# Mamba's first product ahead of the last projection, and depthwise taps moved from VectorE to ScalarE, in a convolution-attention-Mamba-expert kernel

## The chip, the core and the metric

The kernel runs on one core of a Trainium2 chip. A core has a matrix engine (PE, its weight loads shown apart as PEld), a vector engine (DVE), a scalar engine (ACT), a general engine (POOL) and a queue engine (SP) that here only issues transfers. Each works through its own instructions in order and waits on semaphores for the others. SBUF is the on-chip memory, PSUM the eight banks into which PE accumulates, and transfers (DMA) run beside the engines. SP and ACT issue plain transfers; POOL also issues accumulating ones (destination += source).

The metric is device time of one execution in microseconds (us). Each version is run several times, and medians are compared.

## The reference, cut to what matters

An image of 64 x 64 positions and 256 channels passes through three residual layers. `_gn` and `_ln_t` are normalisations without weights.

```python
def _L0_conv_ref(x, W1, W3, W5, Wdw, Wproj, temperature):
    qkv = jnp.concatenate([_conv(xc, W1, 0), _conv(xc, W3, 1), _conv(xc, W5, 2)], axis=1)
    qkv = _conv(qkv, Wdw, 1, groups=3 * c)          # depthwise 3 x 3: nine taps per channel
    q, k, v = jnp.split(qkv, 3, axis=1)
    q, k = (l2n(q), l2n(k))                          # 8 heads of 32 channels, 4096 positions
    attn = jax.nn.softmax(jnp.einsum('bhnc,bhmc->bhnm', q, k) * temperature, axis=-1)
    o = _conv(jnp.einsum('bhnm,bhmc->bhnc', attn, v), Wproj, 0)

def _mamba(x, in_proj_w, conv_w, conv_b, x_proj_w, dt_proj_w, dt_proj_b, A_log, Dp, out_proj_w):
    xc, z = jnp.split(x @ in_proj_w.T, 2, axis=-1)
    xc = silu(causal_conv(xc, conv_w, conv_b))       # 4 taps
    dt, Bm, Cm = split(xc @ x_proj_w.T)              # 16 + 16 + 16
    dt = softplus(dt @ dt_proj_w.T + dt_proj_b)
    h = exp(dt * A) * h + dt * Bm * xc               # a recurrence over 4096 positions
    y = sum(h * Cm) + xc * Dp
    return (y * silu(z)) @ out_proj_w.T

x = x + _L0_conv_ref(_gn(x), ...)
t = t + _L1_attn_ref(_ln_t(t), ...)                  # Mamba forwards + backwards, norm, a two-layer net
t = t + _L1_ffn_ref(_ln_t(t), ...)                   # 2 of 8 experts, gelu, norm
```

All data is float32. Positions are cut into eight chunks of 512, channels into two halves of 128 (`t` or `co`, 0 and 1).

## The kernel before, in words

Four stages follow one another: `conv_phase`, `attention_phase`, `mamba_phase`, `expert_phase`. Nearly all code stands in blocks of `tc.manual_schedule`, in which each engine keeps the order in which Python emits its instructions. Generators are advanced one step at a time (`step`, `drain`), so the order of work is written out by hand. Between two such blocks the compiler merges the engines' two orders, unless an edge between instructions forbids it. A pool (`tc.tile_pool`) hands out a tag's buffers in turn; an instruction that writes a reused buffer waits for the last reader of the old content, a transfer included.

**Convolutions.** k (3 x 3) and v (5 x 5) use Winograd transforms along the width: `inputs` makes the transformed input on DVE, `weights` the transformed weights, which go to DRAM (`uk`, `uv`) and come back as `u`; PE multiplies (L466); `transform_out` brings the products back (`c`, `out_t`, `pad`). q is a plain product (L458). Twelve units (kind, half of the rows, channel half) run in the order k00 k01 k10 k11 q00 v00 q01 v01 q10 v10 q11 v11. Half 0 has 24 output rows, half 1 has 40, since the lower half takes nine rows over from the upper (`edge`, ACT copies at L769 and L807).

`weights(kind, co, dy, r)` takes one row of taps `r` (five times 128 x 256 for v). For v it runs 15 DVE operations of 256 elements in three yields, in tiles of the pool `tp` (six buffers, tag "t"): one for sums `s`, three for results. POOL stores each result pair (L308). The same six buffers serve `c` (L495), the squares `sq` of the norms (L605), `qo` and `vs`.

`depthwise(kind, half, t, pad)` does the nine taps of one unit, in two blocks of rows of 12 (768 elements) or 20 rows (1280). Tap 0 of both blocks is an ACT operation (L559). In the first ten units ACT also computes tap 8 of the second block into `spare` (L564), and POOL adds it to the result by an accumulating transfer (L565). The other taps are DVE operations on the same result (L572), 8 in the first block and 7 in the second, one per step. For v, PE transposes each block as soon as it is done (`turn`, L649 and L651). For q and k the norm follows through `later` and `tick`: `norm_sums` (ACT squares, PE sums), `norm_inverse`, `norm_apply`.

The main loop handles unit n's products and, step by step beside them, unit n-1's depthwise taps: at each group of products it steps `main`, lets PE go on (`feed`, at most three products ahead), calls `tick`, steps the depthwise (6 steps a group for k, 5 for v, all 18 in one go for q) and then `share` pieces of transforms (`step_fill`; twelve in one go for q, before the taps).

**Attention.** For each chunk and channel half, 32 blocks of keys: scores (L1050) into one bank (`ps1`) and three banks (`three()`), exponentials on ACT (L1055, L1056), products with v (L987), sums of exponentials on DVE (L967, L969), accumulated by POOL transfers (L977). `turn` sums them over keys (L1001) and divides; `project` does Wproj, adds the input, stores `x1d` and normalises. The last chunk has its own end: sums, reciprocal (L1006), division (L1025), `project` (L945, L948), store (L950).

**Mamba.** 512 slots, each with two decays on ACT (`da`, L1885), an inflow on POOL (`dbx`, L1895), a scan on DVE (L1908) and a product with C (L1913, some on POOL at L1918), then sums on PE (L1948). Slots of 32 make one chunk and direction. `prepare(q)` makes the next chunk's inputs in 35 steps, one per slot; `LATE` sets other counts for the first 32 slots. The first chunk's inputs are made by `start()`: Silu of `xc` (L1598), first product `pd` (L1607), `xd`, four softplus pieces (`soft` L1617 to L1620, `rest` L1625 to L1627, `log`), `dt_piece` (L1461, L1472, L1476), loads of `b`, `c`, `dtr`, `dtxr` on SP. It also loads the last chunk's `x1` by POOL (L1592) and normalises it to `un` (`layer_norm`), the first input of the backward direction. `start` and the slots advance together: `step(begin)` in each of the first slots.

## Time and profile before

| what | us |
|---|---|
| median of 3 runs (lowest, highest) | 3949.72 (3949.47, 3956.82) |
| profiled execution, its own time | 3948.42 |
| its span | 3946.3 |
| PE busy | 3495.0 (89%) |
| DVE busy | 3308.5 (84%) |
| ACT busy | 2645.8 (67%) |
| POOL busy | 1955.5 (50%) |
| attention's first score (L1050) | at 597.2 |
| last product of attention with v (L987) | ends at 1745.2 |
| first scan (L1908) | at 1787.8 |

Times in the trace are us from the span's start. A line of the timeline gives start, duration of the group, engine, source line, operation, output<-inputs, shape and count; in brackets the idle time of that engine before it and what ended the wait. "issue" is a wait for nothing that the profile shows. The busy shares are means over stages with different limits, so they have to be read stage by stage.

### The profile page before, as it was taken

How to read it: one execution, taken by the hardware profiler on the slowest of the kernel's cores; microseconds unless marked ns; L12 is line 12 of the kernel's file. 1: busy time of each engine (PE TensorE's matmuls, PEld its weight loads, DVE VectorE, ACT ScalarE, POOL GpSimd, SP SyncE). 2: the span in 40 equal slices, each digit the busy share in tenths (PEclk: the TensorE clock that was granted, in tenths of full speed). 3: DMA queues.
4: the chain of work that ended last, by engine and by line, in shares of the span. 5: the costliest groups of instructions: out<-in, count | busy, mean ns of one | idle time of the engine just before them, and what ended most of it. 6: DMA issues, size and time to landing. Idle time of an engine off the chain costs nothing. (4 is left out here: it accounts for less than half of the span.)

```text
span 3946.3 us, 41780 instructions
## 1 busy us (share of the span) xinstructions
PE 3495.0 (89%) x14792; PEld 1121.7 (28%) x14792; DVE 3308.5 (84%) x2391; ACT 2645.8 (67%) x4138; POOL 1955.5 (50%) x1422
## 2 busy tenths in 40 slices
PE   6779999999999999998788888889888888876898
PEld 2334432222222222222222222223222222322444
DVE  8997678888888887778999999999999999999222
ACT  1222338988898898877777778777777777775222
POOL 3121001111111111117889899898988889887000
PEclk9989999999999999998899989989988898988999
DMA  6343246665666665563334433443434345342211
GB/s 217 112 132 104 83 143 141 128 129 112 139 120 121 137 121 118 110 146 122 127 120 124 124 126 117 118 128 118 133 119 121 104 122 152 102 130 79 65 62 57
DMA packets 184186, 471.95 MB, mean 120 GB/s; under 512 B 39205, under 2 KB 48677, under 8 KB 183710
## 3 DMA queue, kind: packets, MB, share of 16 engines
q1 hardware_dynamic: 137166, 304.26, 24.9%
q0 software_dynamic: 44496, 156.53, 19.0%
q10 hardware_dynamic: 2304, 8.39, 0.6%
q8 instruction: 118, 1.93, 0.2%
q14 instruction: 102, 0.84, 0.1%
HBM read 268.17 MB, written 79.56 MB: 88 GB/s over the span
## 5 line engine op out<-in xcount | busy, mean ns | idle before, releaser
L1895 POOL TENSOR_TENSOR dbx<-dtxr,b 128x1024 f32<-128x1024 f32 x512 | 1203.1, 2359 | 194.3 <-DVE da L1908 104.4
L1908 DVE TENSOR_TENSOR_SCAN da<-da,state,dbx 128x1024 f32<-128x1024 f32 x432 | 1014.0, 2347 | 15.7 <-ACT da L1885 7.1
L1056 ACT ACTIVATE e<-sc 128x1536 f32<-128x1536 f32 x512 | 740.2, 1446 | 1.3 <-PE sc L1050 1.3
L1885 ACT ACTIVATE da<-dtr,aneg 128x512 f32<-128x512 f32 x1024 | 708.1, 692 | 32.9 <-DMA dtr<-dtd 2.4
L977 POOL DMA_DIRECT2D s<-s x222 | 194.0, 999 | 900.6 <-DVE s L969 523.3
L969 DVE TENSOR_TENSOR s<-s,e 128x2048 f32<-128x2048 f32 x256 | 586.7, 2292 | 44.1 <-ACT e L1056 20.7
L1050 PE MATMUL sc<-q,kS 32*128 32x512 f32 x4096 | 588.3, 639 | 4.6 <-ACT e L1055 3.9
L1913 DVE TENSOR_TENSOR h<-da,c 128x1024 f32<-128x1024 f32 x432 | 529.2, 1225 | 32.5 <-DVE da L1908 0.5
L987 PE MATMUL av<-e,vT 128*32 128x512 f32 x4096 | 545.4, 605 | 2.4 <-DVE o L993 2.4
L1948 PE MATMUL y<-h,sel 128*32 128x512 f32 x2048 | 377.5, 663 | 93.1 <-DVE h L1913 68.1
L466 PE MATMUL cv<-v,u 128*128 128x512 f32 x928 | 410.3, 603 | 37.8 <-DVE pad L287 13.6
L967 DVE TENSOR_TENSOR s<-e 128x2048 f32<-128x2048 f32 x128 | 293.2, 2291 | 127.5 <-ACT e L1056 110.0
L1055 ACT ACTIVATE e<-sc 128x512 f32<-128x512 f32 x512 | 305.9, 597 | 112.8 <-PE sc L1050 58.1
L1341 PE MATMUL mm<-u,win 128*128 128x512 f32 x464 | 243.9, 667 | 69.9 <-ACT z L1449 28.9
L1050 PEld LDWEIGHTS sc<-q,kS 32*128 32x128 f32 x4096 | 163.8, 183 | 430.7 <-ACT e L1055 387.6
L1939 ACT COPY state<-da 128x2 f32<-128x2 f32 x431 | 68.7, 160 | 300.9 <-DVE h L1913 297.4
L466 PEld LDWEIGHTS cv<-v,u 128*128 128x128 f32 x928 | 178.3, 193 | 267.0 <-issue 222.3
L572 DVE SCALAR_TENSOR_TENSOR acc<-pad,wdw_s,acc 128x768 f32<-128x768 f32 (+1 forms) x182 | 224.8, 1240 | 33.3 <-ACT acc L559 27.9
L1387 PE MATMUL mm<-xp,taps 128*128 128x512 f32 x480 | 213.3, 596 | 0.6 <-DVE m L1537 0.6
L1908 DVE TENSOR_TENSOR_SCAN h<-da,state,dbx 128x1024 f32<-128x1024 f32 x80 | 187.5, 2343 | 10.3 <-ACT state L1939 9.3
L987 PEld LDWEIGHTS av<-e,vT 128*32 128x32 f32 x4096 | 80.9, 108 | 390.9 <-issue 376.7
L1918 POOL TENSOR_TENSOR h<-h,c 128x1024 f32<-128x1024 f32 x80 | 188.3, 2353 | 1.0 <-ACT state L1939 1.0
(380 smaller groups left out, 3894.1 us busy)
## 6 DMA issues: line engine op xcount, KB each, us to landing
s<-s POOLq DMA_DIRECT2D x222, 512.0 KB, 6.4
dtr<-dtd SPq DMA_DIRECT2D x128, 512.0 KB
dtxr<-dtd SPq DMA_DIRECT2D x128, 512.0 KB
b<-bcd SPq DMA_DIRECT2D x64, 256.0 KB
c<-bcd SPq DMA_DIRECT2D x64, 256.0 KB
dtd<-dt SPq DMA_DIRECT2D x64, 256.0 KB
dtd<-few SPq DMA_DIRECT2D x64, 256.0 KB
u<-uv SPq DMA_DIRECT2D x24, 640.0 KB
```

The costliest lines, as they stand in the source:

```text
L466: nc.tensor.matmul(rows4(ps), u[:, dy, P * ci : P * ci + P], v[:, dy : dy + HR, ci, :], start=dy + ci == 0, stop=dy == k - 1 and ci == CT - 1,
L967: nc.vector.tensor_tensor(g.part, before, e, ALU.add)
L969: nc.vector.tensor_tensor(g.part, g.part, e, ALU.add)
L987: nc.tensor.matmul(g.av[32 * h : 32 * h + 32, :], vT[:, kb, P * t + 32 * h : P * t + 32 * h + 32], e[:, h, :], start=kb == 0, stop=kb == N ...
L1050: nc.tensor.matmul(sc[1][:, h - 1, :] if h else sc[0], kS[r, t, P * kb : P * kb + P], q_t[r, t, :], start=True, stop=True,)
L1055: nc.scalar.activation(e[:, 0, :], sc[0], AF.Exp)
L1056: nc.scalar.activation(e[:, 1:4, :], sc[1], AF.Exp)
L1885: nc.scalar.activation(da[:, v, :], dts[i, e, j][0][:, v, :], AF.Exp, scale=aneg[i % 2][:, a : a + 1])
L1895: nc.gpsimd.tensor_tensor(u, dts[i, e, j][1], bcs[i, k][0][:, None, :].to_broadcast([P, 2, N]), ALU.mult)
L1908: nc.vector.tensor_tensor_scan(das[n].rearrange("p v n -> p (v n)"), da.rearrange("p v n -> p (v n)"), u.rearrange("p v n -> p (v n)"), st ...
L1913: nc.vector.tensor_tensor(h, da, bcs[i, k][1][:, None, :].to_broadcast([P, 2, N]), ALU.mult)
L1948: nc.tensor.matmul(ys[i, e][32 * j : 32 * j + 32, :], cx.sel, hs[n + j // 2][:, j % 2, :], start=False, stop=k == SQ - 1,)
```

## The change

Three things are changed.

1. In the first ten units `depthwise` hands taps 7 and 8 of both blocks to ACT (`aside`): ACT writes each into a scratch tile (`spare`, and `spare2` or a free part of the result for half 0), POOL accumulates it. The second block's pair goes first, the first block's after its DVE taps. DVE keeps six taps a block. The transposes of v come after both blocks. The edges of q move to DRAM tiles (`q_edges`), stored and reloaded by POOL.
2. `weights` works on two arrays at once (512 elements) where it can. For v that makes ten operations instead of 15, and six buffers instead of four; stores and yields stay three pairs and three.
3. At the end of attention the sums and the last projection use the single bank (`alone()`), and the projection is emitted last. `start()` adds two compile-time edges: the projection's first product comes behind the first softplus product on PE, its first addition behind `dt_piece` on DVE. `pd` uses another bank. Six of the seven steps of `un`'s norm move from before the first slot into the slots, and `LATE` starts `prepare(1)` later. Pool `b_w` is placed before `b_sm`.

```diff
@@ conv_phase
-        edges = {
-            k: one.tile([P, 9, 4, TX], FP, name=f"edge{i}") for i, k in enumerate((0, 1, ("q", 0), ("q", 1)))
-        }
+        edges = [one.tile([P, 9, 4, TX], FP, name=f"edge{t}") for t in range(CT)]
+        q_edges = [cx.rows.tile([P, 9, 4, TX], FP, name=f"q_edge{t}", tag=f"q_edge{t}") for t in range(CT)]
...
         def weights(kind, co, dy, r):
...
+            s, o = two(), two()
             if kind == "v":
-                plus(y, w[1], w[3])
-                plus(x, x, w[4])
-            plus(o[:, 0, :], x, y if kind == "v" else w[1])
-            plus(o[:, 1, :], x, y if kind == "v" else w[1], ALU.subtract)
-            store()
-            yield
...
+                plus(s, r[:, 0:2, :], r[:, 2:4, :])
+                plus(s[:, 0, :], s[:, 0, :], r[:, 4, :])
+                odd = s[:, 1, :]
...
+            plus(o[:, 0, :], s[:, 0, :], odd)
+            plus(o[:, 1, :], s[:, 0, :], odd, ALU.subtract)
+            store(o, (0, 1))
+            yield
...
+            s, odd, o = two(), two(), two()
+            madd(s, r[:, 4::-4, :], 4.0, r[:, 2:3, :].to_broadcast([P, 2, C]))
+            madd(s, s, 4.0, r[:, 0:5:4, :])
+            madd(odd, r[:, 3:0:-2, :], 4.0, r[:, 1:4:2, :])
+            yield
+            for f, points in ((2.0, (2, 4)), (-2.0, (3, 5))):
+                if f < 0:
+                    o = two()
+                madd(o, odd, f, s)
+                store(o, points)
+            yield
...
+            def aside(b):
+                m = mine * W // 2
+                for tap, x in ((7, spare), (8, spare2 if half else dst[:, 2 * m : 3 * m])):
+                    _, src, w_ap = piece(b, tap)
+                    x = x[:, 0:m]
+                    nc.scalar.activation(x.rearrange("p (h w) -> p h w", w=W), src, AF.Copy, scale=w_ap)
+                    nc.gpsimd.dma_start(out=dst[:, m * b : m * b + m], in_=x, accum_op=ALU.add)
             if away:
-                o, src, w_ap = piece(1, 8)
-                x = spare[:, 0 : mine * W // 2]
-                nc.scalar.activation(x.rearrange("p (h w) -> p h w", w=W), src, AF.Copy, scale=w_ap)
-                nc.gpsimd.dma_start(out=dst[:, mine * W // 2 : mine * W], in_=x, accum_op=ALU.add)
+                aside(1)
...
-                for tap in range(1, 8 if b and away else 9):
+                for tap in range(1, 7 if away else 9):
...
-                if kind == "v":
-                    m = mine * W // P // 2
-                    turn(dst, t, row0 * W // P, m * b, m, ("tr", "ps2") if shared else ("tr",))
+                if away and b == 0:
+                    aside(0)
+                m = mine * W // P // 2
+                for part in (range(2) if b else ()) if away else (b,):
+                    if kind == "v":
+                        turn(dst, t, row0 * W // P, m * part, m, ("tr", "ps2") if shared else ("tr",))
...
-                    nc.scalar.copy(pad[:, 0:9, 1:5, :], edge)
+                if half and kind == "q":
+                    nc.gpsimd.dma_start(out=pad[:, 0:9, 1:5, :], in_=q_edges[t])
+                elif half:
+                    nc.scalar.copy(pad[:, 0:9, 1:5, :], edges[t])
...
-                    nc.scalar.copy(edge, pad[:, LAG : LAG + 9, 1:5, :])
+                if not half and kind == "q":
+                    nc.gpsimd.dma_start(out=q_edges[t], in_=pad[:, LAG : LAG + 9, 1:5, :])
+                elif not half:
+                    nc.scalar.copy(edges[t], pad[:, LAG : LAG + 9, 1:5, :])
@@ attention_phase
+        def alone():
+            return ps1.tile([P, N], FP, name="sc1", tag="sc1")
...
-                ps = aside()
+                ps = alone() if c == NCH - 1 else aside()
...
+                    if c == NCH - 1 and co + t == 0:
+                        behind.append(ins)
+                ins = nc.vector.tensor_tensor(x1[:, co, :], xr[:, co, :], ps, ALU.add)
+                if c == NCH - 1 and co == 0:
+                    behind.append(ins)
...
-            den = three()[:, 0, :]
+            den = alone() if g.last else three()[:, 0, :]
...
+            for task in queue:
+                drain(task)
             drain(turning)
-            for task in queue + [project(NCH - 1, oT)]:
-                drain(task)
+            drain(project(NCH - 1, oT))
+    return behind
@@ mamba_phase, start()
-            pd = mm_psum()
+            pd = tl_psum()
...
+            def ahead_of(ins):
+                tc.add_manual_dep(
+                    ins.ins, next(i for i in reversed(nc.cur_bb.bb.instructions) if i.engine == ins.ins.engine).name,
+                    mybir.DependencyInfo(mybir.DependencyClass.NoSync, mybir.DependencyReason.DATA), reason="behind",
+                )
             soft(0)
+            if behind:
+                ahead_of(behind[0])
             rest(0)
             log(0)
             for v in range(2):
                 dt_piece(0, v, 0, ex, nc.vector)
+                if behind and v == 1:
+                    ahead_of(behind[1])
...
-            step(norm)
-            step(norm)
             soft(1)
-            step(norm)
             soft(2)
             rest(1)
             soft(3)
-            step(norm)
...
             inflow(1)
-            step(norm)
             load_bc(0, 3)
             yield
+            step(norm, 3)
...
             step(norm)
-            nc.sync.dma_start(out=ud[NCH - 1], in_=un)
-            drain(norm)
             yield
             dt_piece(0, 0, 2, ex)
             yield
             dt_piece(0, 1, 2)
+            step(norm)
             yield
...
             dt_piece(0, 0, 3, ex)
             yield
+            step(norm)
+            nc.sync.dma_start(out=ud[NCH - 1], in_=un)
+            drain(norm)
             dt_piece(0, 1, 3)
...
-        LATE = {0: 0, 1: 0, 2: 0, 3: 0, 5: 2, 6: 2, 7: 5, 15: 2, 16: 2, 17: 2}
+        LATE = {0: 0, 1: 0, 2: 0, 3: 0, 4: 0, 5: 0, 6: 2, 7: 3, 8: 3, 9: 3, 10: 2, 15: 2, 16: 2, 17: 2}
```

## The prediction

> **What bounds the kernel now.** I read the page's busy shares first, then the busy time by stretch (a stretch from:to, its length, then busy time of PE, PEld, DVE, ACT and POOL, PE's clock, DMA share, GB/s):
>
> ```profile
> 127.00:204.00 77.00, 62.58 (x153) 25.78 (x153) 73.55 (x73) 19.96 (x30) 4.64 (x8) 0.90 0.33 98
> 204.00:274.00 70.00, 53.01 (x127) 21.31 (x126) 62.17 (x91) 19.67 (x30) 19.29 (x34) 0.89 0.46 146
> 274.00:306.00 32.00, 32.00 (x79) 13.29 (x82) 31.27 (x49) 4.83 (x8) 6.53 (x12) 0.94 0.34 122
> 306.00:598.00 292.00, 274.61 (x694) 117.45 (x691) 206.69 (x201) 93.28 (x143) 25.32 (x48) 0.97 0.35 112
> 598.00:1746.00 1148.00, 1140.16 (x8449) 271.03 (x8448) 934.63 (x489) 1016.91 (x1065) 205.17 (x234) 1.00 0.62 125
> 1746.00:1788.00 42.00, 32.16 (x56) 10.11 (x56) 29.64 (x59) 16.95 (x25) 5.88 (x4) 0.76 0.59 203
> 1900.00:3655.00 1755.00, 1465.78 (x4132) 470.98 (x4130) 1690.29 (x1030) 1310.76 (x2580) 1534.48 (x934) 0.90 0.40 119
> ```
>
> So: in the convolutions DVE is the bound up to about 274, with PE idle 14.4 and 17.0 us in the first two rows; from 274 PE is (32.00 of 32, then 274.61 of 292); attention is PE's (1140 of 1148); the scans are DVE's (96%). Between attention and scans lies a fill of 42 us in which nobody is full. Next, PE's timeline over the convolutions: where PE waits, it waits for DVE's evacuations of PSUM.
>
> ```profile
> 126.60 17.98 PE L466 MATMUL cv<-v,u 128*128 128x512 f32 x36 [13.59 <-DVE pad L287]
> ...
> 203.37 5.13 PE L458 MATMUL cv<-xpad,wq 128*128 128x512 f32 x8 [14.42 <-DVE pad L287]
> ...
> 273.82 19.47 PE L466 MATMUL cv<-v,u 128*128 128x512 f32 x40 [9.68 <-DVE out_t L290]
> ```
>
> What DVE does ahead of those evacuations are depthwise taps and weight transforms; its timeline shows a transform held by its own stores, and the 15 taps of unit (k,1,1) in one run:
>
> ```profile
> 230.40 0.76 DVE L287 SCALAR_TENSOR_TENSOR wo<-wx 128x256 f32<-128x256 f32 x2 [1.71 <-DMA uv<-wo]
> ...
> 248.85 23.71 DVE L572 SCALAR_TENSOR_TENSOR acc<-pad,wdw_s,acc 128x1280 f32<-128x1280 f32 x15
> ```
>
> Last the timeline of the fill. Mamba's first product (L1607) has its input by 1748.9 and starts at 1760.43, behind the projection; from there a fixed chain runs to the first scan:
>
> ```profile
> 1750.88 3.36 DVE L1006 RECIPROCAL rs<-sc 128x512 f32<-128x512 f32 x1 [2.74 <-PE sc L1001]
> ...
> 1760.43 3.60 PE L1607 MATMUL mm<-xc,wx 128*48 128x512 f32 x8 [0.87 <-DVE x L948]
> ...
> 1770.91 0.33 SPq L1476 DMA_DIRECT2D dtd<-dt  x1
> ...
> 1781.73 4.87 POOL L1895 TENSOR_TENSOR dbx<-dtxr,b 128x1024 f32<-128x1024 f32 x2 [17.06 <-DMA dtxr<-dtd]
> 1781.81 2.58 DVE L1625 TENSOR_SCALAR few<-ex 128x512 f32<-128x512 f32 x1
> ...
> 1787.80 2.35 DVE L1908 TENSOR_TENSOR_SCAN da<-da,state,dbx 128x1024 f32<-128x1024 f32 x1
> ```
>
> **Part 1: taps to ScalarE.** Ten of twelve units lose 3 of 15 DVE taps: 18 x 1.018 us (768 elements) and 12 x 1.551 us (1280), 36.9 us of DVE. ACT gains 18 x 0.92 + 12 x 1.35 = 32.8 us, POOL 30 issues x 0.89 = 27 us, and 30 more accumulating transfers land. ACT (44 of 179 us busy from 127 to 306) and POOL (30 of 179) have room. Only taps ahead of a PE wait count. Units (k,0,0) and (k,0,1): 3 x 1.02 each, out of the 14.4 us wait, 6.1. Unit (k,1,0): 3 x 1.55 = 4.65, out of the 9.68 wait. Unit (q,0,0) runs where PE is full: nothing; cover is PE's v products, and with it gone it would be worth 3.
>
> Unit (k,1,1) pays part back. Its second block must wait for two accumulations onto the same bytes. The first issues at 249.96 after the weight stores on POOL, and lands 5.8 us later (measured there). If the second waits for it: 0.9 issue and about 5 (the others: 3.8 to 6.6), so 261.6. The first block's six taps end at 248.85 + 6 x 1.58 = 258.3: a stall of 3.3, net gain 4.65 - 3.3 = 1.35. Ends: no waiting between them, gain 4.65; landings of 6.6, gain 0. The Trainium skill, "DMA: Bandwidth & Descriptors", Rules for kernel authors, says that an accumulating DMA must be waited for before another touches the same bytes. The same page, Anatomy of one DMA, puts the fixed cost of any DMA at about 2 us; with 2 in place of 5 for the second landing, the stall would be 0.3 and the total 3 us better. The trace's rows, 3.8 and more, say otherwise.
>
> After 306 PE decides. Its 4.75 us wait at 393 (for DVE's pad) loses two taps of unit (q,0,1): -2. Units (v,0,0), (v,0,1) and (v,1,0) run their taps in one go, under 26 us of PE's v products, and PE's transposes follow. Their two blocks now both end with four accumulations in a row. For (v,1,0): spare at 498.45, then 4 x (0.9 + 5.1) less overlap, lands about 516.5, against transposes that start at 514.74 and today wait 1.95 in the middle: +1 (0 to +5). For the 768 ones 3.8 each, end 336.5 against 341.15: covered with 4.6 to spare.
>
> The q edges go through DRAM: four ACT copies (0.67) off, four POOL issues on. The reload is needed about 5 us after its pad is free; nearest rows land in 2.5 (256 KB stores) and 8.4 us (384 KB loads): 0, up to +3 each. Who waits is ACT's side copies and behind them the taps, under the same 26 us.
>
> **Part 2: weight transforms.** A v transform takes 5.65 us today in 15 operations (0.34 to 0.45 apart at 256 elements). The new one has ten, of them six at 512 (0.60 to 0.68 apart): 5.25. Five for v0 ahead of 126: -2. For v1, four run from 219.5 to 248.85, with 6.1 us of stalls for stores. They share six buffers with the norm's squares, three of which PE holds until 235 (it reads them at 234.18). Today a transform needs four buffers, then six; the last pair can only reuse the one whose store has just left. With stores landing in 2 to 7 us I get +3 and +2 in the first two transforms, -1 in each of the others: +3 (ends: -8, 21 us without stalls; +10, 4 us more in three).
>
> Convolutions: -6.1 - 4.65 - 1.35 - 2 + 3 = -11.1 up to 274, then -2 + 1: **-12** (ends -27 and +4). PE's waits there (13.6 + 14.4 + 9.7 alone) are large enough to give it.
>
> **Part 3: Mamba's start.** L1607 goes behind the softmax sums, which end at 1750.82: 9.6 earlier. Its bank is now that of the attention output, copied out by 1747.7. The 21.3 us from its start to the first inflow on POOL stay: 1772.1, and 2.43 later, at 1774.6, the scan has its inputs. Today it starts 3.6 after that point, since DVE has the last two softplus rests first, slowed from 0.42 to 2.58 and from 0.69 to 2.73 beside POOL. With the projection's two adds (0.69 each) behind dt_piece and the norm's subtraction gone from there, these rests end between 1770 (softplus products ahead of the projection's second half on PE) and 1778 (behind it: that half waits for the first add, as both have one bank). I take 1775.5, near the inputs: 12.3 earlier; ends 9 and 13.2.
>
> What is moved: the projection's eight matmuls (about 4 us) run in PE time free after 1756; its adds cost DVE 1.4 where DVE waits for ACT anyway. The x1 store on SP leaves near 1764.6 instead of 1760.3. POOL's load of x1 waits for it (3.8 today) in front of the first inflow: 1768.4 against 1772.1, so a slip above 3.7 delays the scan one for one. Six of the norm's seven steps go into the slots: subtraction 1.22 on DVE, which is full there: +1.2. Square 1.04 and reciprocal-root row 0.66 on ACT fit its idle 1.9 per slot; pow 1.24 and the product 2.33 on POOL (two inflows ahead), 3.8 on PE and four issues on SP are covered by the scans. Uncovered, POOL's would cost 1.2 (the product is there today). The second direction's preparation starts two slots later, with the same total of 37 steps; today's waits of the first 32 slots (about 10 us, most for ACT's da) move, and I count 0, from -3 to +4. The setup's taps and skips (5.2 us of DVE) have about 5 us of waiting to fall into; uncovered +3.
>
> Mamba: -12.3 + 1.2: **-11** (ends -15 and -4). Afterwards DVE stays the bound, so the shift reaches the end.
>
> **Sum.** -23. The profiled execution took 3948.42 (span 3946.3 and 2.1 around it), 1.3 under the median 3949.72. It would be 3925.4, by the median 3926.7: 3927.
>
> **Rivals.** (a) The convolutions give nothing: v1's buffers and the accumulations eat it (-12 becomes 0 to +2): 3939 to 3941. For: the 6.1 us of store waits already there. Against: (k,0,0) to (k,1,0) have their landings 10 us ahead of need. (b) Mamba's head start is lost, since the compile-time order leaves L1607 behind the projection, or x1's load blocks POOL: -12 and -1 remain: 3937. For: POOL's queue has that load ahead of the inflow. Against: 3.7 us of slack. (c) Slower: the accumulations land later beside one another. Place: the end of (v,0,0), (v,0,1), (v,1,0) before PE's transposes, and (k,1,1). Each us of landing costs 4 in (v,1,0), 4 in the 768 units above their 4.6 of slack, 2 in (k,1,1). Two us more (7 instead of 5) cost 8 + 3 + 3 + 4 = 18, nearly all of the gain; four cost 16 + 11 + 11 + 8 = 46: 3973. It decides from about 2.3 us. For: the landings spread from 3.8 to 6.6 with single transfers. Against: the DMA share is 0.35 there.
>
> **How the numbers follow.** Forecast 0.56 (its own range 3915 to 3938), (a) 0.20, (b) 0.13, (c) 0.11. 0.2% (7.9 us) is about what a measurement tells from no change. Faster: all of the forecast and (b), nearly half of (a) and none of (c): 0.77; same: the rest of (a) and the start of (c), 0.14; slower 0.09. The range takes the forecast's low side with the better ends (no stalls in v1, -40: 3910) and reaches over (a) and (b) to 3948.
>
> **What would show it.** PE's waits at 203 and 273 shorter by 6 and 5 with L572 at 12 per unit; a wait of DVE for DMA inside (k,1,1); the stores' waits in v1; attention's first score near 585 instead of 597. L1607 right behind L1001, the first scan 43 us after the last exp becoming about 31. The prediction is wrong if accumulations wait on each other for longer than 5 us, if PE's transposes of v wait, or if the first 32 slots lose what the start gained.

## The result, and the profile after

The changed kernel takes 3966.01 us (median of 7 runs, 3960.57 to 3970.61), the kernel before, run beside it, 3951.95 us (7 runs). The ratio is 1.0038 with a 95% interval of 1.0029 to 1.0047: 14 us slower, where 23 us faster were forecast. The profiled execution took 3966.26 us with a span of 3964.3, which is 18.0 more than the span of before. Repeated executions of the kernel before lay between 3938.9 and 3957.5 us over all the comparisons below, so single profiles are compared by landmarks inside them, and times by their medians and intervals.

Two landmarks cut the loss in two. The first is attention's first score on PE, where the convolutions end: 597.22 before, 605.43 after (+8.2). The second is the fourteenth scan, from which on all scans keep their distance for 40 and more: 1838.47 before, 1853.54 after (+15.1), of which 7.4 are there already at attention's last run of products (1742.06 and 1749.42). So the convolutions lost 8.2 us instead of gaining 12, and Mamba's start lost 7.7 instead of gaining 11. Later single waits of scans make 15.1 into 18.6 in this one profile; the medians differ by 14.1.

The stretches of the profile after, with the same columns as the prediction's table (busy time of PE, PEld, DVE, ACT and POOL, PE's clock, DMA share, GB/s), their bounds moved with the landmarks:

```profile
125.00:202.00 77.00, 62.31 (x153) 25.85 (x154) 67.74 (x67) 26.04 (x35) 11.25 (x17) 0.90 0.55 142
202.00:275.00 73.00, 54.94 (x127) 22.76 (x128) 55.45 (x66) 21.35 (x29) 22.92 (x38) 0.84 0.56 160
306.00:606.00 300.00, 278.36 (x688) 119.38 (x686) 187.43 (x184) 105.70 (x153) 41.09 (x66) 0.94 0.48 136
1753.00:1785.00 32.00, 18.81 (x40) 5.17 (x40) 25.06 (x58) 13.75 (x20) 2.88 (x2) 0.73 0.68 239
```

DVE did lose work (73.55 to 67.74 us in the first row, 62.17 to 55.45 in the second), but these stretches are no shorter (77 and 70 us before). The work left DVE and the time stayed. The last row shows that the fill between attention and the scans did shrink, from 42 to 32 us.

PE's timeline after, where it waits in the convolutions, and attention's first score. Most of these waits are for an evacuation, the operation on DVE or ACT that reads a finished PSUM bank and so frees it for PE:

```profile
125.27 17.68 PE L470 MATMUL cv<-v,u 128*128 128x512 f32 x36 [11.68 <-DVE pad L286]
...
201.75 6.67 PE L462 MATMUL cv<-xpad,wq 128*128 128x512 f32 x8 [14.42 <-DVE pad L286]
...
262.01 10.71 PE L470 MATMUL cv<-v,u 128*128 128x512 f32 x20 [18.06 <-ACT c L499]
...
522.49 1.09 PE L663 MATMUL ps<-ident,acc 128*128 128x128 f32 x4 [5.98 <-DVE acc L583]
...
605.43 1.12 PE L1075 MATMUL sc<-q,kS 32*128 32x512 f32 x2
```

The wait of 13.6 us shrank by 1.9; that of 14.42 is the same to the hundredth, although six taps of 1.02 were to come out of it. The wait of 9.68 for DVE at 274 is gone, but PE now stands 18.06 us for an ACT copy at 262, and it goes on at 274.70 where it did at 273.82. At 522 there is a new wait of 5.98.

Behind the wait for ACT, in DVE's and ACT's timeline of the profile after:

```profile
230.93 0.69 DVE L286 SCALAR_TENSOR_TENSOR wx<-wx 128x512 f32<-128x512 f32 x1 [4.31 <-DMA uv<-wx]
...
247.47 9.48 DVE L583 SCALAR_TENSOR_TENSOR acc<-pad,wdw_s,acc 128x1280 f32<-128x1280 f32 x6
...
254.55 1.36 ACT L572 ACTIVATE spare<-pad,wdw_s 128x1280 f32<-128x1280 f32 x1 [37.79 <-DMA acc<-spare]
...
260.12 1.36 ACT L572 ACTIVATE spare<-pad,wdw_s 128x1280 f32<-128x1280 f32 x1 [4.21 <-DMA acc<-spare]
260.13 9.55 DVE L583 SCALAR_TENSOR_TENSOR acc<-pad,wdw_s,acc 128x1280 f32<-128x1280 f32 x6 [3.18 <-DMA acc<-spare]
261.39 0.56 ACT L499 COPY c<-cv 128x512 f32<-128x512 f32 x1
```

ACT's tap for the first block must wait until the transfer that still reads the scratch tile has landed. The copy of PE's finished bank (c) stands behind it in ACT's order: PE had that bank ready at 244, ACT copies it at 261.39. The Trainium skill, "PSUM — Partial Sum Buffer", Engine vs sequencer instructions, says that ScalarE's queue is strictly first in, first out; these lines agree.

At 522 it is unit (v,1,0). POOL's and DVE's timeline after:

```profile
500.44 0.89 POOL L573 DMA_DIRECT2D acc<-spare  x1 [5.11 <-ACT spare L572]
506.04 0.88 POOL L573 DMA_DIRECT2D acc<-spare  x1 [4.71 <-issue]
507.69 0.86 POOL L573 DMA_DIRECT2D acc<-spare  x1 [0.78 <-DVE acc L583]
...
512.91 9.55 DVE L583 SCALAR_TENSOR_TENSOR acc<-pad,wdw_s,acc 128x1280 f32<-128x1280 f32 x6 [5.76 <-DMA acc<-spare]
...
517.20 0.86 POOL L573 DMA_DIRECT2D acc<-spare  x1 [8.65 <-DMA acc<-spare]
```

The second accumulation onto the second block is issued 5.60 us after the first, when that has landed, and lands 6.9 us later. Only then do the block's six taps begin, 5.76 us late; they end at 522.46, and PE's transposes start at 522.49. The first block, which PE transposes first, is ready no earlier: its second accumulation is issued at 517.20, when the one ahead of it has landed, and lands 5.2 us later, at 522.4. The profile puts PE's wait down to the taps, but the two ends lie 0.1 us apart. The Trainium skill, "DMA: Bandwidth & Descriptors", Rules for kernel authors, demands that an accumulation waits for the one before it onto the same bytes, and the trace shows it kept.

Last, Mamba's start after, from the timelines of PE, SP, DVE and POOL:

```profile
1757.73 3.63 PE L1634 MATMUL tl<-xc,wx 128*48 128x512 f32 x8
...
1771.27 0.33 SPq L1503 DMA_DIRECT2D dtd<-dt  x1
...
1785.05 2.36 DVE L1943 TENSOR_TENSOR_SCAN da<-da,state,dbx 128x1024 f32<-128x1024 f32 x1 [2.25 <-ACT da L1920]
...
1815.40 2.35 POOL L149 TENSOR_TENSOR un<-ln_xc,ln_rstd 128x1024 f32<-128x1024 f32 x1 [0.29 <-DMA ln_rstd<-ln_inv]
...
1829.26 10.57 PE L1414 MATMUL mm<-xp,taps 128*128 128x512 f32 x24
...
1847.53 2.35 DVE L1943 TENSOR_TENSOR_SCAN h<-da,state,dbx 128x1024 f32<-128x1024 f32 x1 [5.33 <-ACT da L1920]
```

Counted from attention's last run of products, the first product starts 10.0 us earlier than before and the first scan 10.1 earlier. Then the product that makes the norm's result un starts at 1815.40 (1796.22 before), the second direction's products follow in one run of 10.57 us, and the tenth to the fourteenth scan wait for ACT and for PE's y sums. Of the 10.1 us nothing is left by then: 17.8 are lost in fourteen slots, 7.0 of them in the first four scans and 11.0 from the tenth on.

### The profile page after: what moved, and what is told of

It is laid out like the page before. It is cut to its first block, busy times and chain, and to the rows that moved or that the text cites. A ratio compares the mean times of both kernels' runs of the same rounds, so it can differ in the third digit from the quotient of the medians.

```text
span 3964.3 us, 41756 instructions
## 1 busy us (share of the span) xinstructions
PE 3496.7 (88%) x14792; PEld 1124.8 (28%) x14792; DVE 3263.7 (82%) x2301; ACT 2674.3 (67%) x4164; POOL 1985.6 (50%) x1456
## 5 line engine op out<-in xcount | busy, mean ns | idle before, releaser
L583 DVE SCALAR_TENSOR_TENSOR acc<-pad,wdw_s,acc 128x768 f32<-128x768 f32 (+1 forms) x152 | 188.4, 1243 | 65.1 <-ACT acc L564 33.7
```

## The experiments

The first theory, from the traces alone: (A) the convolutions lose through the taps, by two accumulations onto one block; Mamba loses because x1 comes late and the norm, un and the second direction's preparation with it. The rivals are in the expectations. The table gathers the landmarks of all runs: shift of attention's first score and of the fourteenth scan against the profile of before, the latter also counted from attention's last run of products, and the ratio of times to the kernel before.

| run | first score | 14th scan | 14th scan, from attention's end | ratio (95% interval) |
|---|---|---|---|---|
| the change | +8.2 | +15.1 | +7.7 | 1.0038 (1.0029 to 1.0047) |
| e1_taps | +8.0 | +7.1 | +0.2 | 1.0004 (0.9994 to 1.0014) |
| e2_weights | +6.6 | +5.5 | -1.0 | 1.0006 (0.9994 to 1.0017) |
| e3_mamba | 0.0 | +9.7 | +9.4 | 1.0019 (1.0008 to 1.0031) |
| e4_x1_early | +0.9 | +2.6 | +1.2 | 1.0003 (0.9993 to 1.0014) |
| e5_v_single | 0.0 | -2.8 | -1.9 | 0.9993 (0.9983 to 1.0004) |
| e6_pace | +7.7 | +7.3 | -0.9 | 1.0011 (1.0000 to 1.0021) |
| e7_bufs8 | -6.1 | -7.7 | -0.6 | 0.9980 (0.9971 to 0.9990) |
| e8_act_setup | +3.2 | +3.7 | -0.2 | 0.9992 (0.9983 to 1.0002) |
| e9_norm_late | -0.6 | +12.3 | +13.6 | 1.0032 (1.0020 to 1.0045) |
| e10_bufs_only | -0.3 | -0.9 | -0.4 | 0.9993 (0.9984 to 1.0003) |
| e11_bufs8_act | -6.6 | -8.1 | -2.9 | 0.9980 (0.9968 to 0.9991) |
| e12_taps_k | -7.2 | -6.3 | +1.8 | 0.9965 (0.9952 to 0.9978) |
| e13_late_only | +2.1 | +9.0 | +6.9 | 1.0014 (1.0004 to 1.0023) |
| e14_norm_only | -0.5 | +6.9 | +7.4 | 1.0016 (1.0007 to 1.0025) |
| e15_best | -7.9 | -12.8 | -3.7 | 0.9956 (0.9943 to 0.9970) |

Single profiles scatter. The six runs that leave the convolutions as they were (e3, e4, e8, e9, e13, e14) have the first score between -0.6 and +3.2; up to 2.4 us come in before 110 us, where DVE waits for the first weights and their stores (0.80 us of waiting at 83 before, 2.68 in e1_taps). The seven that leave Mamba's start as it was (e1, e2, e5, e6, e7, e10, e12) have the fourteenth scan, counted from attention's end, between -1.9 and +1.8. A single profile does not tell a difference inside these bounds from nothing.

**Parts alone.** e1 is the diff's taps and edges, e2 its `weights`, e3 its hunks in `attention_phase` and `mamba_phase`, each on the kernel before.

> The kernel before with the change's taps alone (two taps of nine per block on ScalarE, the q edges through DRAM); weight transforms and Mamba's start as before. Theory A, read from the two traces: the convolutions lose time through the accumulations (the two onto one block run one after the other, ACT stands still behind its scratch, PE's transposes of unit (v,1,0) wait), so the taps alone move attention's first score from 597.2 to between 604 and 608, and the time rises by 7 to 11 us, to about 3960. Rival B: the weight transforms cost it, with their wide tiles in the buffers shared with the norm; then the taps alone leave the first score at 597 or below, and the time within 2 us of before.

> The kernel before with the change's weight transforms alone. Theory A: PE's first wait in the convolutions goes from 13.6 to about 11.7 us, the transforms of v1 wait as long for their stores as before, and what is left at attention's first score is 0 to 1.5 us earlier than 597.2; the time is 0 to 2 us below before. Rival B (the weight transforms cost the convolutions): first score at 603 or later, time 6 us or more above before.

> The kernel before with the change's Mamba start alone (first product ahead of the last projection, norm steps among the slots, second direction's preparation later). Theory A: the first scan starts 9 to 11 us earlier than 1787.8 and by the fourteenth scan the kernel is 6 to 9 us behind the kernel before (15 to 18 us lost among the first 14 slots), which stays to the end: time 6 to 9 us above before. Rival C: the parts act on each other only together (the convolutions' delay shifts what meets at the start); then the Mamba start alone keeps its gain, and the time is 5 to 10 us below before.

e1 shows what theory A says of the first score, with PE's wait of 6.37 us at 522 again; 2.4 of its 8.0 us are the chance named above, and by the ratio its time is only 1.6 us (-2.4 to +5.5) above before, not the 7 to 11 expected. e2 goes by rival B: the first score is 6.6 late, and DVE waits 11.8 us for stores and 4.4 ahead of the fourth transform (6.1 in all before); its time, too, rises by less than rival B says (2.4 us by the ratio). So both parts move the first score on their own, by separate causes, and both together by no more than one alone. e3 is nearly as theory A expects (the fourteenth scan 9.7 behind instead of 6 to 9, the time 7.5 above by the ratio), and rival C falls.

**x1 early.** On e3: the first x1 add ahead of the softplus, the second behind the dt pieces, the norm's steps a slot earlier, the table LATE of before.

```
+            if behind:
+                ahead_of(behind[1])      # right behind aneg
...
-        LATE = {0: 0, 1: 0, 2: 0, 3: 0, 4: 0, 5: 0, 6: 2, 7: 3, 8: 3, 9: 3, 10: 2, 15: 2, 16: 2, 17: 2}
+        LATE = {0: 0, 1: 0, 2: 0, 3: 0, 5: 2, 6: 2, 7: 5, 15: 2, 16: 2, 17: 2}
```

> The run of the Mamba start alone, with three things put elsewhere: the projection's two adds on DVE go ahead of the softplus (the first) and right behind the first dt pieces (the second), so that the x1 store leaves some 4 us earlier and ahead of the dtr load; the norm's steps are one slot earlier each; the second direction's preparation starts as early as in the kernel before. Theory A (x1 comes late, and through it the norm, un and the preparation): first scan 12 to 14 us earlier than 1787.8, un's product at 1800 or before, fourteenth scan 3 to 8 us ahead of the kernel before, time 3 to 8 us below before. Rival D: the preparation's work on PE and ACT meets the scans wherever x1 is, because the scans now start before it; then the fourteenth scan is 4 us or more behind as in the run of the Mamba start alone, and the time 3 to 8 us above before.

The loss is gone but for 1.2 us, which is inside the scatter; the gain did not come, so neither theory A's range nor rival D's was met. As three things were changed at once, this run cannot say which of them did it; e9, e13 and e14 show what the steps' places cost.

**One tap aside in v units.** The change's taps and weights, Mamba's start as before. In the v units the transposes also go back behind each block:

```
-                for tap in range(1, 7 if away else 9):
+                for tap in range(1, (8 if b else 9) if one_tap else 7 if away else 9):   # one_tap: v units
...
-                if away and b == 0:
+                if away and b == 0 and not one_tap:
                     aside(0)
```

> The change's taps and weight transforms (Mamba's start as before), but the v units keep one tap on ScalarE and one accumulation, as before. Theory A (the taps cost the convolutions through the two accumulations onto one block of v units, which PE's transposes wait for): PE's wait of 6.0 us at 522 falls below 1 and attention's first score, 605.4 with the whole change, comes to between 597 and 600; time about 6 below that of taps and weights together, within 2 us of before. Rival E (the loss lies ahead of that, in the scratch that holds ACT from 254 to 261, and is only collected at 522): the first score stays at 603 or later.

PE's timeline at the transposes of (v,1,0), first of the kernel before, then of e5_v_single, then of e1_taps:

```profile
514.74 0.66 PE L649 MATMUL ps<-ident,acc 128*128 128x128 f32 x4
```

```profile
514.14 0.66 PE L665 MATMUL ps<-ident,acc 128*128 128x128 f32 x4
...
519.18 1.09 PE L665 MATMUL ps<-ident,acc 128*128 128x128 f32 x4 [1.74 <-issue]
```

```profile
521.86 1.09 PE L658 MATMUL ps<-ident,acc 128*128 128x128 f32 x4 [6.37 <-DMA acc<-spare]
```

The transposes start at 514 as in the kernel before, and all 8.2 us are back at the first score. Theory A holds for the convolutions, rival E falls: the scratch holds ACT here too (PE waits 18.87 us at 262), and the first score is that of before. e5 takes away both things that end at 522 in the change, the late taps and the late landing, so it does not say which of them counts; in e1 the profile puts PE's wait down to the landing.

**The pace of the taps.** The change's taps and weights with `-(-12 // groups)` in place of `-(-18 // groups)` in the loop over the units, which is the number of `step(before)` per group.

> The change's taps and weight transforms (Mamba's start as before), with the taps paced at four steps per group of output rows in the k units instead of six (three instead of five in v units). Theory F: the removed taps were the last of each unit, behind PE's waits, and six steps still lie ahead of each evacuation; at four steps PE's wait of 11.7 us at 125 shrinks by about 2 us (2 x 1.02) and that of 14.4 us at 202 by about 3 us (2 x 1.56), so PE reaches 205 some 5 us earlier than with the whole change; the time falls by 0 to 5 us against taps and weights together, since the v transforms behind can take some back. Rival G (PE's waits are not set by the taps ahead of the evacuation but by what the transforms of the output wait for): both waits change by less than 1 us.

PE's timeline of e6_pace:

```profile
194.86 6.42 PE L462 MATMUL cv<-xpad,wq 128*128 128x512 f32 x8 [8.77 <-DVE pad L286]
...
257.62 10.91 PE L470 MATMUL cv<-v,u 128*128 128x512 f32 x20 [20.82 <-ACT c L499]
...
398.99 3.78 PE L470 MATMUL cv<-v,u 128*128 128x512 f32 x4 [8.14 <-ACT pad L793]
...
521.95 1.08 PE L663 MATMUL ps<-ident,acc 128*128 128x128 f32 x4 [6.06 <-DVE acc L583]
```

The wait of 14.42 fell to 8.77 and the one ahead of it from 11.68 to 9.91: theory F, with a larger effect than the 3 us expected of the second. DVE runs a fixed six steps of the unit before ahead of each evacuation, however many taps are left; a shorter unit only ends sooner behind it. Of the 6.9 us at 195 only 4.4 are left at 257, where ACT's scratch takes its share. The rest is gone at 429, ahead of the double accumulation: at 399 PE waits 8.14 us for ACT's copies into `pad`, and these wait 10.04 us for a depthwise tap on DVE. This run slowed the taps in v units as well, to three steps per group, and they now end there.

**Buffers.** e7 is e2 with `bufs=8` instead of 6 in the pool a_t and the q edges through DRAM, for room; e10 is the same on the weight transforms of before.

> The change's weight transforms alone with eight buffers of 2 KB per partition instead of six in the pool they share with the norm; for the room the two q edges go through DRAM as in the change. Theory A2 (the wide tiles wait for their own stores because the pool is small): DVE's waits for stores in v1's transforms, 16.2 us with the weight transforms alone (6.1 in the kernel before), fall to 6 us or less, the six-tap run of unit (k,1,1) starts at 246 or before instead of 255.5, and attention's first score comes to between 590 and 597 instead of 603.8; time 3 to 8 us below before. Rival H (the waits are the stores' own landing time on a loaded queue, and more buffers are used up by the norm's squares): waits of 10 us or more remain, first score 600 or later.

> The kernel before with eight buffers in the shared pool and the q edges through DRAM, and its own weight transforms of 256 elements. Theory A2' (buffers are what v1's transforms lack, and the wide transforms are worth about 2 us of DVE): the waits for stores in v1 fall from 6.1 to below 3 us, attention's first score comes to between 592 and 596 (597.2 before), time 1 to 6 us below before, and some 3 us above the run with wide transforms and eight buffers. Rival J (all of that run's gain is the buffers'): first score 589 to 592, time 6 to 10 us below before.

DVE's timeline in the transforms of v1, first of e2_weights, then of e7_bufs8:

```profile
230.27 0.69 DVE L287 SCALAR_TENSOR_TENSOR wx<-wx 128x512 f32<-128x512 f32 x1 [6.55 <-DMA uv<-wx]
...
239.58 1.29 DVE L287 SCALAR_TENSOR_TENSOR wx<-wx 128x512 f32<-128x512 f32 x2 [4.59 <-DMA uv<-wx]
...
255.54 23.71 DVE L577 SCALAR_TENSOR_TENSOR acc<-pad,wdw_s,acc 128x1280 f32<-128x1280 f32 x15
```

```profile
227.95 0.69 DVE L286 SCALAR_TENSOR_TENSOR wx<-wx 128x512 f32<-128x512 f32 x1 [1.14 <-DMA uv<-wx]
...
233.19 0.69 DVE L289 TENSOR_TENSOR wx<-wr 128x512 f32<-128x512 f32 x1 [4.55 <-DMA wr<-in_w]
...
243.62 23.71 DVE L576 SCALAR_TENSOR_TENSOR acc<-pad,wdw_s,acc 128x1280 f32<-128x1280 f32 x15
```

With two more buffers the waits fall from 16.2 to 5.7 us, most of what is left being the load of the next raw weights, and the taps start 11.9 us earlier. The time falls by 0.20% (0.10 to 0.29): rival H falls. The buffers alone (e10) leave 3.5 us of store waits and move neither the first score nor, beyond its interval, the time: a miss for the expectation of 592 to 596, and rival J falls too. It also has e7's way of the q edges through DRAM, which therefore is not the gain. By the first score, the wide transforms and the buffers are worth something only together (+6.6, -0.3, and -6.1 with both); by time, the intervals of e7 and e10 still overlap.

**Setup on ACT.** On e4: the 24 scaled identities (tap matrices of the second direction, skip matrices) are built by ACT in its gaps instead of by DVE ahead of the softplus.

```
-                nc.vector.tensor_scalar(tp[:, j, :], cx.ident, cx.col(f"convw{d}", j), None, ALU.mult)
+                nc.scalar.activation(taps[1][:, j, :], cx.ident, AF.Copy, scale=cx.col("convw1", j))
```

> The run with x1 early, with the second direction's tap matrices and the skip matrices (24 operations, 5 us of DVE ahead of the softplus) built on ACT in its idle time. Theory A3 (the setup on DVE delays dt, x1 and through them first scan and preparation): against the last attention product, the first scan comes 3 us earlier than in the run with x1 early (from 36.8 us to about 33.5 behind the start of the last run of attention products) and the fourteenth scan 2 to 4 us earlier; time 2 to 5 us below before. Rival D2 (from the fifth scan on the second direction's preparation on ACT and PE paces the scans, whenever they begin): the first scan is 3 us earlier and the fourteenth within 1 us of the run with x1 early.

The first scan came 2.5 us earlier, the fourteenth 1.4: between A3 and D2, though 1.4 is inside the scatter, and the intervals of the times of e4 and e8 overlap. Counted from attention's end, un comes 1.4 earlier too (55.1 us against 56.5), and DVE waits 5.66 us ahead of the sixth scan for an inflow that stands on POOL behind un's product.

**The moves among the slots.** e9 is the kernel before with the change's places of the norm's steps and its table LATE, but the first product behind the projection as before; e13 only the table; e14 only the norm's steps. In e14 the first eight products of the second direction's projection (at 1805.18) read un before the norm's last product has written it (at 1812.12), so their wait for un is missing from its time; the next eight do wait for it.

> The kernel before with the second half of the change's Mamba start alone: the norm's steps among the slots and the second direction's preparation later, while the first product stays behind the projection. Theory A4 (the preparation, which starts from the norm's un, sets the pace from the fifth slot on; the later steps cost about 18 us over 14 slots, from which the head start of 10 is then taken off): the first scan stays within 2 us of 1787.8 or gains up to 6 (the norm is out of its way), un's product ends more than 15 us later than 1798.5, the fourteenth scan is 10 to 18 us behind the kernel before, and the time 9 to 17 us above. Rival I (the loss comes from the head start itself, by x1's late store, and not from the steps' new places): the fourteenth scan is within 4 us of the kernel before, the time too.

> The kernel before with the change's table of preparation steps per slot alone (second direction's preparation from the seventh slot on, three steps per slot in slots 7, 8 and 9); norm and first product where they were. Theory L (the steps, crowded into few slots, put up to 10.6 us of the preparation's products on PE ahead of the y sums and hold ACT's decays): the first seven scans stay within 1 us of the kernel before, and the fourteenth is 8 to 14 us behind; time 6 to 14 us above before. Rival N (the cost is the norm's, whose steps hold ACT and POOL in the first slots): the fourteenth scan within 3 us of before, time too.

> The kernel before with the norm's steps among the slots alone; first product and the preparation's table as before. Theory L: the first scan 3 to 5 us earlier (the norm is out of its way, as with the later preparation), the next four lose that again; the preparation then waits for un, and the fourteenth scan is 2 to 8 us behind before. Rival N: the fourteenth scan 10 us or more behind before.

From PE's, DVE's and ACT's timelines of e13_late_only:

```profile
1823.23 10.57 PE L1387 MATMUL mm<-xp,taps 128*128 128x512 f32 x24
...
1832.54 2.36 DVE L1908 TENSOR_TENSOR_SCAN da<-da,state,dbx 128x1024 f32<-128x1024 f32 x1 [1.90 <-ACT da L1885]
...
1833.84 0.69 ACT L1383 ACTIVATE xc<-mm,small 128x512 f32<-128x512 f32 x1 [1.38 <-PE mm L1387]
1839.32 0.69 ACT L1383 ACTIVATE xc<-mm,small 128x512 f32<-128x512 f32 x1 [4.80 <-PE mm L1387]
...
1839.99 1.42 ACT L1885 ACTIVATE da<-dtr,aneg 128x512 f32<-128x512 f32 x2
1841.49 2.35 DVE L1908 TENSOR_TENSOR_SCAN h<-da,state,dbx 128x1024 f32<-128x1024 f32 x1 [5.33 <-ACT da L1885]
...
1847.51 2.36 DVE L1908 TENSOR_TENSOR_SCAN da<-da,state,dbx 128x1024 f32<-128x1024 f32 x1 [3.66 <-ACT da L1885]
```

ACT's timeline of the kernel before at the same copies:

```profile
1826.85 0.69 ACT L1383 ACTIVATE xc<-mm,small 128x512 f32<-128x512 f32 x1 [2.44 <-PE mm L1387]
...
1830.28 0.69 ACT L1383 ACTIVATE xc<-mm,small 128x512 f32<-128x512 f32 x1 [1.15 <-PE mm L1387]
...
1830.95 1.42 ACT L1885 ACTIVATE da<-dtr,aneg 128x512 f32<-128x512 f32 x2
```

The waits of e13 are the changed kernel's (0.69, 1.90, 5.33, 3.66) with nothing else changed but three steps per slot in slots 7 to 9: 24 products of 10.57 us on PE ahead of the y sums, and behind them ACT's copies, in whose order the decays of the next scans stand. The table of before has a slot of five steps, but three of these emit nothing; its products come in two runs of 16 (7.14 us each), and one copy stands ahead of each decay. In e13 three of its steps with products share a slot, and two copies stand ahead of a decay.

From PE's and DVE's timelines of e14_norm_only:

```profile
1790.01 3.43 PE L122 MATMUL tl<-un,mean_mat 128*128 128x512 f32 x4 [8.39 <-ACT un L131]
...
1799.65 2.36 DVE L1906 TENSOR_TENSOR_SCAN da<-da,state,dbx 128x1024 f32<-128x1024 f32 x1 [3.51 <-ACT state L1937]
...
1814.51 6.54 PE L1341 MATMUL mm<-un,win 128*128 128x512 f32 x8 [4.94 <-POOL un L149]
...
1823.51 2.36 DVE L1906 TENSOR_TENSOR_SCAN da<-da,state,dbx 128x1024 f32<-128x1024 f32 x1 [5.09 <-ACT da L1883]
```

Here the norm's sums stand on PE, waiting for its square, ahead of products that ACT copies before its next decays, and the fourth scan waits; later the second direction's products wait for un, ACT's copies for them, and the ninth scan for ACT.

Counted from attention's end, the table costs 6.9 us, the norm's steps 7.4, both together 13.6; by the ratios 0.14%, 0.16% and 0.32%. So theory L holds in the main for both runs, and rival N falls: in e13 the fourteenth scan is 9.0 behind, inside theory L's range, the time 5.5 us above, just under it (and the sixth scan 2.3 behind, where 1 was the bound). x1's store leaves as early in e9 as before, so the late store, which theory A blamed, is not needed for the loss. Rival I falls, and theory A is wrong in this half. The head start then takes off 4.2 (9.4 in e3 against 13.6), not 10; why it is not more is open.

**Repaired versions.** e11 joins e7 and e8. e12 is e7 with taps aside in k units only: taps 7 and 8 of both blocks in (k,0,0) and (k,0,1), tap 8 of both blocks in (k,1,0), and `-(-(12 if kind == "k" else 18) // groups)` steps. e15 joins e12 and e8.

> The wide weight transforms with eight buffers together with the Mamba start that has x1 early and the setup on ACT. If the two parts add up: first score about 591, time 8 to 12 us below before. If the preparation paces the first scans whatever comes ahead of it, the Mamba part adds nothing: 6 to 8 us below.

> The wide weight transforms with eight buffers, and of the change's taps only those of the k units, paced at four per group: two taps per block aside in units (k,0,0) and (k,0,1), one per block in (k,1,0), all others as before. Theory F (what counts is how many taps lie ahead of PE's evacuations): PE's waits of 11.4 and 14.4 us fall to about 9.5 and 9 us, PE reaches 205 some 6 us earlier than in the run with eight buffers alone, and attention's first score comes to between 584 and 588 (591.1 there); time 10 to 15 us below before. Rival K (the v1 transforms behind them take it back, since they wait for weights to load and for stores): first score 589 or later, time as with eight buffers alone.

> Wide weight transforms with eight buffers, the taps of the k units at four per group, and the Mamba start with x1 early, the setup on ACT and the preparation's table as before. If the parts add up: first score at 590, fourteenth scan 8 to 9 us ahead of the kernel before, time 10 to 16 us below before (0.25 to 0.4%). If the Mamba start adds nothing, it equals the run with the k taps, 9 to 14 us below.

e11 is as fast as e7; its Mamba part, 2.9 us at the fourteenth scan, does not show in the time. e12 reaches 195.19 at the second wait, 5.8 us earlier than e7 as theory F expects, but only 1.1 of it is left at the first score, as rival K says (3.69 us of waiting for raw weights at 237, PE's wait of 10.55 at 267 as in e7). Its time is nevertheless 0.35% below before (0.22 to 0.48), more than that landmark; the intervals of e7 and e12 overlap, so the surplus over e7 is not settled. e15 has the lowest median: 0.44% (0.30 to 0.57) below before, 3933.5 us against 3950.3, a little more than expected; its interval overlaps that of e12. Timelines of e15_best:

```profile
194.63 5.52 PE L462 MATMUL cv<-xpad,wq 128*128 128x512 f32 x8 [10.21 <-DVE pad L286]
...
1741.88 3.63 PE L1648 MATMUL tl<-xc,wx 128*48 128x512 f32 x8
...
1766.24 2.36 DVE L1953 TENSOR_TENSOR_SCAN da<-da,state,dbx 128x1024 f32<-128x1024 f32 x1 [5.16 <-POOL dbx L1940]
...
1784.69 2.36 POOL L149 TENSOR_TENSOR un<-ln_xc,ln_rstd 128x1024 f32<-128x1024 f32 x1 [3.19 <-DMA ln_rstd<-ln_inv]
```

Counted from attention's end, the fourteenth scan is 3.7 us earlier here, beyond the scatter in runs with the old start (-1.9 to +1.8), but in time e15 is not told from e12. un comes 51.8 us behind attention's last run of products, 54.2 in the kernel before and 66.0 in the change.

## Why the prediction was wrong, point by point

- *What bounds the kernel*: half right. DVE's work fell where it was said to bind; but what sets PE's two large waits is not how much DVE has to do, only what of it stands ahead of the evacuation.
- *Units (k,0,0) and (k,0,1), 6.1 us out of the 14.4 us wait*: wrong, 0. The removed taps were the last of a unit, behind the evacuation; six steps per group stay ahead. e6 showed it by changing the pace alone: 5.7 us out of that wait.
- *Unit (k,1,0), 4.65, and (k,1,1), 1.35*: the stall of 3.3 us was measured as 3.18, right. The gain of 4.65 was taken back by store waits in v1 (four waits and one for raw weights, 13.2 us). That ACT would be held by the reuse of its scratch was not in the working; PE went on 0.9 us later, though e5, with the same hold, ends its convolutions no later than before.
- *After 306: -2 and +1 (0 to +5)*: the wait at 397 lost 1.7 us, right; the v units with 768 elements stayed covered, right. Unit (q,1,0), counted at nothing, lost 2.2 in this profile, where its two accumulations held DVE for 10.02 us at 460; in e1, with the same taps, it lost nothing. The +1 for (v,1,0) became +6.2, outside its ends. The sum there took some 6 us off for overlap and had the last transfer land at 516.5; it landed at 522.4. The four landings took 5.1, 6.8, 9.0 and 5.2 us where 5.1 each was reckoned, and each pair ran one behind the other. The sum also left out that the second block's six taps start only after both of its landings. With landings of 5.1 these taps would have ended at about 520.7 (an estimate from the trace's rows: 506.04 + 5.1 + 9.55), so some 4 of PE's 6 us are the order of taps and landings, and the rest is later landings: rival (c), which named the place and that cause, is right in part. The prediction set the fixed 2 us of the Trainium skill, "DMA: Bandwidth & Descriptors", Anatomy of one DMA, against its rows; with that page's term for the bytes, 640 KB would land after 3.5 us (an estimate by the page). Going by the rows was right, but the rows of single transfers were too low as well.
- *v0's weights -2*: 1.3 to 1.8, right. *v1's weights +3 (-8 to +10)*: +7.7 alone (from 1.1 ahead at 202 to 6.7 behind at 280), within its ends, and the buffers named there are the cause: e7. The new transform has nine operations, not ten (six of 512 elements, three of 256); it takes 5.2 us (from 242.35 to 247.55), near the 5.25 reckoned.
- *The first product 9.6 earlier, the first scan 12.3 earlier (9 to 13.2)*: 10.0 and 10.1, inside the ends. The x1 store left 8.8 us later than before, counted from attention's end, where 4.3 were reckoned; bringing it forward (e4) did not move the first scan. The setup's taps and skips on DVE came out on the uncovered side that was priced at +3: 2.5 us at the first scan in e8.
- *The norm's steps +1.2, the later preparation 0 (-3 to +4)*: the step that failed most. Without the head start the two cost 13.6 us (e9), singly 7.4 and 6.9. The prediction counted the steps' total, which is the same, and set the work on PE, ACT and POOL against idle time there; it didn't look at what stands behind a step in order: products behind the norm's sums on PE (e14), decays behind two copies on ACT (e13).
- *The shift reaches the end*: right, for the loss: after the fourteenth, the scans keep their distance.
- *Rivals*: (a) had the convolutions give nothing; they lost 8.2. (b) was wrong as to cause: the head start was there, and was lost over the fourteen slots behind it. The sum: 20.2 us off in the convolutions (+8.2 for -12) and 18.7 in Mamba (+7.7 for -11) stand against the 39 us between forecast and measurement.

Open: how much of e1's and e2's losses is there in every execution, since by the ratios they lie 1.6 and 2.4 us above before, with intervals of some 4 us to either side, and their profiled spans 8.2 and 3.7; and whether e12's gain over e7 is its taps or its pace, since 15 taps at four steps were not run; and which of the two ends at 522, taps or landing, holds PE in the change.

## What to carry to other kernels

Work taken off a bounding engine helps only if it stood ahead of what the others wait for: find the last instructions before the wait and check that these are what goes; where work is metered in steps per stage, the meter must shrink with it. When steps are moved between slots, price the slot that gets most work, with everything that stands behind it in order on each engine, not the sum. A second accumulation onto the same bytes adds its landing to the path of whatever comes after both; and a wider instruction needs the buffers to match, or its stores take the gain back.

## What was not expected of the hardware

- Two accumulating transfers of 640 KB onto one block cost 5.60 and 6.9 us one behind the other in (v,1,0), and 8.9 us from issue to issue in (q,1,0) (443.35 and 452.29). A third, issued onto the other block of (v,1,0) while the second was on its way, took 9.0; the single one there took 5.1 in the kernel before.
- The same load of x1 (512 KB) landed 4.0 us after issue in the kernel before and 6.7 us after it in e8, where the dt, b and c loads run beside it.
- The rests of the softplus on DVE, slowed to 2.58 and 2.73 us beside POOL's inflows before, run in 0.42 and 0.69 in the change, where they come ahead of them.
